# A product stage that centers and projects in one matmul per token on half of the array's rows

## The chip, the cores and the metric

The kernel runs on one core of one Trainium2 chip. The metric is the device time of one execution in microseconds (us); the lower the better. The times given are the median of several executions; the profile is of one execution, with its own time.

## The reference

The input `x` is 512 x 512 positions of 64 channels, in f32. Two layers are each added to their input.

Layer 0 first applies a group norm, then a triangle product over one axis of positions:

```python
xn = _ln(x, norm_w, norm_b)
left = xn @ left_w + left_b          # masked, times sigmoid(xn @ lgate_w + lgate_b)
right = xn @ right_w + right_b       # the same with its own weights
out = einsum('bkjd,bkid->bijd', left, right)
out = _ln(out, onorm_w, onorm_b)
out = out @ out_w + out_b
return out * sigmoid(xn @ ogate_w + ogate_b)
```

Layer 1 is a group norm, a two-dimensional Fourier transform cut to 12 x 12 modes, a complex matrix product over the channels for each mode, and the inverse transform.

The part that matters here is the line `out = _ln(out, onorm_w, onorm_b)` with the projection by `out_w` after it. For one token (one position with 64 channels), the layer norm subtracts the mean over its channels (centering), needs the sum of squares of the centered values, and divides by a root. Because the root is one number per token, the kernel projects the values first (with weights that have the centering folded in) and multiplies by the factor afterwards: `z = (token @ w_out) * rs + bias`, where `rs` is one over the root of the mean square of the centered token.

## The kernel before, in words

Rows whose mask is zero give nothing to the product, so the kernel compacts the rows with a mask to at most 256 (`compact`). Its stages follow one another:

- the masked rows are gathered, transposed for statistics and kept in SBUF (lines 640 to 690);
- they are normed and projected to left and right, 64 rows of the array at a time (L746), and written to DRAM;
- for each of the 64 channels, left and right are read back, transposed and multiplied (L835, L849); the product lies in the SBUF tile `places`, with 128 partitions for positions and, along the free axis, tokens of 64 channels;
- the stage with the change (lines 857 to 1141), described below;
- the layer 1 stage: modes, inverse transform and the sum, written to the output (lines 1143 to 1270).

The stage with the change works on groups of 64 tokens per partition, each group in 8 steps of 8 tokens per partition. `first` is 8: the first 8 groups (64 steps) hold the product and give `u`, the projected and normed product, which is written to DRAM (`u_d`). The 32 groups after them (256 steps) hold gathered tiles of `x`; they give the output gate, are multiplied by `u` or by the bias row, added to `x`, and stored. The names are: `transpose(s)` (L918) turns 8 tokens per partition with four transposes of 128 x 128 into the PSUM tile `t_ps`, and ScalarE copies it to the SBUF tile `xt_c` (L927; L929 for the later groups). In `xt_c` the array's rows 0 to 63 hold the channels of the even token of a pair and rows 64 to 127 those of the odd one. `times` (L931) multiplies such a tile, as the stationary operand, by a 128 x 128 matrix with two equal 64 x 64 blocks on the diagonal: four matmuls (L934). It is called twice per step: by `centered` (L937) with the matrix `center`, into `c_ps`, and by the loop (L1058) with `w_out`, into `w_ps`; the later groups use `center_x` and `gate_x`.

ScalarE squares `c_ps` (L944) into `sq_c`, of which there are two buffers of two steps each; VectorE sums the squares per token (L948), ScalarE takes the root once per group (`root`, L954), and VectorE the reciprocal (L1106). VectorE then multiplies `w_ps` by the factor into `z_t` (L1112) and, for two steps together, adds the bias, which is kept in PSUM (L1115); SyncE's queue stores `z_t` to `u_d` (L1118).

The order of the work is written out by hand in the loop at L1047: each engine takes its instructions in the order in which this loop issues them. A round `s` transposes step `s + 13` (`LEAD` is 13), projects step `s`, centers and squares step `s + 12`, sums the squares up to step `s + 11`, and scales step `s`. The loop begins at `s = -13`, so 13 rounds transpose and center before the first projection. The projection thus comes 12 rounds after the centering of the same tile, and for that time the tile waits in a ring of 15 buffers (L895). PSUM has eight banks: two for `t_ps`, two for `c_ps`, two for `w_ps`, one for sums and bias rows (`scratch`), one for the modes (`f_ps`).

```python
if s + LEAD < total_g:
    transpose(s + LEAD)
if 0 <= s < total_g:
    wps = times(ps_w, "w_ps", s, weights["out"] if k < first else gate_x)
if 0 <= s + LEAD - 1 < total_g:
    cps = centered(s + LEAD - 1)
...
if cps is not None:
    squared(s + LEAD - 1, cps)
```

Of the kernel before, what the change touches and what calls it, by code (L numbers as in the profile page):

```python
# [9 lines left out]
F32 = mybir.dt.float32  # L10
I32 = mybir.dt.int32
AF = mybir.ActivationFunctionType
ALU = mybir.AluOpType
AX = mybir.AxisListType
PSUM = bass.MemoryType.PSUM
DRAM = bass.MemoryType.DRAM

P = 128
N = 512
C = 64  # L20
# [26 lines left out]
def conv_preact_kernel(ctx: ExitStack, tc: tile.TileContext, t: dict):  # L47
    nc = tc.nc
    x, out = t["x"], t["out"]
# [12 lines left out]
    def load_const(name, shape):  # L62
        c = const.tile(shape, F32, name=name)
        nc.scalar.dma_start(c, t[name])
        return c

    ident = load_const("c_ident", [P, P])
    center = load_const("c_center", [P, P])
# [13 lines left out]
    with tc.tile_pool(name="ix", bufs=1) as xp, tc.tile_pool(  # L82
        name="ixp", bufs=1, space=PSUM
# [51 lines left out]
    weights, biases = {}, {}  # L135
# [476 lines left out]
    def compact(fc):  # L612
# [31 lines left out]
        with tc.tile_pool(name="xc", bufs=1) as cp:  # L644
            xc = cp.tile([P, K + 1, 2, C], F32, name="xc")
            with tc.tile_pool(name="f1", bufs=1) as sp, tc.tile_pool(name="f1x", bufs=2) as xp, tc.tile_pool(
                name="f1y", bufs=4
# [19 lines left out]
                for jc in range(NJ):  # L667
                    if jc % quarter == 0:
                        stats = sp.tile([P, 1, 16 * quarter, 6], F32, name="stats1c")
                    for r in range(4):  # L670
                        flat = xgs[jc][1][r].rearrange("p j c -> p (j c)")
                        for c in range(4):

                            ps = pt.tile([P, 4, P], F32, name="x_ps")
# [18 lines left out]
            with tc.tile_pool(name="fb", bufs=QB + 8) as gp, tc.tile_pool(name="fw", bufs=2) as wk, tc.tile_pool(  # L693
                name="fr", bufs=3
            ) as rp, tc.tile_pool(name="fg", bufs=1) as sp, tc.tile_pool(name="fo", bufs=2) as op, tc.tile_pool(
                name="fpt", bufs=2, space=PSUM
            ) as pt, tc.tile_pool(name="fpc", bufs=1, space=PSUM) as pc, tc.tile_pool(
                name="fpp", bufs=1, space=PSUM
# [13 lines left out]
                def centered(q):  # L712
                    cps = pc.tile([P, 8, C], F32, name="cc_ps")
                    for i in range(4):
                        nc.tensor.matmul(
                            cps[:, 2 * i : 2 * i + 2, :], gts[q][:, i * P : (i + 1) * P], center, start=True, stop=True
                        )
                    sq = wk.tile([P, 8, C], F32, name="sqc")
                    nc.scalar.activation(sq, cps, AF.Square)
                    k, n = divmod(q, QB)  # L720
                    if n == 0:
                        totals[k] = rp.tile([P, QB * 8], F32, name="total")
                    return sq, totals[k][:, 8 * n : 8 * n + 8]
# [26 lines left out]
                for q in range(-QB - 6, groups):  # L750
# [14 lines left out]
                    if live(QB + 5):  # L765
                        sq, total = centered(q + QB + 5)
# [22 lines left out]
        with tc.tile_pool(name="rb", bufs=2) as rp, tc.tile_pool(name="rbp", bufs=2, space=PSUM) as rps:  # L789
            for name in ("ogate", "out"):  # L790
                wide = rp.tile([P, P], F32, name="wide_" + name, tag="wide")
                nc.vector.tensor_copy(wide, biases[name].to_broadcast([P, P]))
                ps = rps.tile([P, C], F32, name="row_" + name, tag="row")
# [6 lines left out]
        center_x = fc.tile([P, P], F32, name="center_x")  # L800
        gate_x = fc.tile([P, P], F32, name="gate_x")
# [4 lines left out]
        with tc.tile_pool(name="tri", bufs=1) as trp:  # L806
# [17 lines left out]
            with tc.tile_pool(name="ti", bufs=4) as ip, tc.tile_pool(name="tt", bufs=3) as tp, tc.tile_pool(  # L824
                name="tpt", bufs=4, space=PSUM
            ) as ps_t, tc.tile_pool(name="tpo", bufs=3, space=PSUM) as ps_o:
                for c in range(C):
                    sides = []
                    for name, src in (("left", left_d), ("right", right_d)):
                        raw = ip.tile([P, 2, K], F32, name=name + "_raw")  # L830
# [15 lines left out]
                    ps = ps_o.tile([P, 2, K], F32, name="tri_c_ps")  # L846
# [10 lines left out]
            SIZE = 8  # L857
            LEAD = 13
            RING = 5
            first = K * 2 // 64  # L860

            units = [(jc, half) for jc in range(NJ) for half in ((1, 0) if jc < NJ - 1 else (0, 1))]
            total_g = (first + len(units)) * SIZE
            with tc.manual_schedule(), tc.tile_pool(name="late", bufs=1) as lp:
# [11 lines left out]
                def place(i):  # L876
                    return places[:, i * 64 * C : (i + 1) * 64 * C].rearrange("p (n c) -> p n c", c=C)
# [14 lines left out]

                    (nc.gpsimd if h == 3 else nc.sync).dma_start(modes_t, modes_d[h * P : (h + 1) * P])

                with tc.tile_pool(name="np_x", bufs=LEAD + 2) as tp, tc.tile_pool(name="np_q", bufs=2) as sqp, tc.tile_pool(  # L895
                    name="np_s", bufs=3
                ) as small, tc.tile_pool(name="oz", bufs=4) as zp, tc.tile_pool(
                    name="o1", bufs=1
                ) as s1, tc.tile_pool(name="np_t", bufs=2, space=PSUM) as ps_t, tc.tile_pool(
                    name="np_c", bufs=2, space=PSUM  # L900
                ) as ps_c, tc.tile_pool(name="np_w", bufs=2, space=PSUM) as ps_w, tc.tile_pool(
                    name="np_n", bufs=1, space=PSUM
                ) as ps_n, tc.tile_pool(name="opf", bufs=1, space=PSUM) as ps_f:
                    scratch = ps_n.tile([P, 4, P], F32, name="scratch")
                    sum_ps = [scratch[:, 3, i * G : (i + 1) * G] for i in range(2)]
                    bias_ps = {"out": scratch[:, 2, :C], "ogate": scratch[:, 2, C:]}
# [5 lines left out]
                    xts, rss, sqs, us, zs, fs, st = {}, {}, {}, {}, {}, {}, {}  # L912
                    last = len(units) - 1

                    def x_of(k):
                        return place(order[k % RING])

                    def transpose(s):  # L918
                        k, n = divmod(s, SIZE)
                        flat = (place(k) if k < first else x_of(k - first)).rearrange("p n c -> p (n c)")  # L920
                        tps = ps_t.tile([P, 4, P], F32, name="t_ps")
                        for i in range(4):
                            o = (8 * n + 2 * i) * C
                            nc.tensor.transpose(tps[:, i, :], flat[:, o : o + P], ident)  # L924
                        xts[s] = tp.tile([P, 4, P], F32, name="xt_c")
                        if k < first:
                            nc.scalar.copy(xts[s], tps)  # L927
                        else:
                            nc.scalar.activation(xts[s], tps, AF.Identity, bias=ab1[:, 2:3])  # L929

                    def times(pool, name, s, w):  # L931
                        ps = pool.tile([P, 8, C], F32, name=name)
                        for i in range(4):
                            nc.tensor.matmul(ps[:, 2 * i : 2 * i + 2, :], xts[s][:, i, :], w, start=True, stop=True)  # L934
                        return ps

                    def centered(s):  # L937
                        return times(ps_c, "c_ps", s, center if s < first * SIZE else center_x)

                    def squared(s, cps):  # L940
                        n = s % SIZE
                        if n % 2 == 0:
                            sqs[s // 2] = sqp.tile([P, 16, C], F32, name="sq_c")
                        nc.scalar.activation(sqs[s // 2][:, 8 * (n % 2) : 8 * (n % 2) + 8, :], cps, AF.Square)  # L944

                    def summed(s):
                        k, n = divmod(s, SIZE)
# [32 lines left out]
                    def finished():  # L980

                        z = zs.pop((last, 3))
                        made = [ps_c.tile([P, 8, C], F32, name="c_ps") for _ in range(2)]
                        for i, ps in enumerate(made):
                            u = bias_ps["out"].unsqueeze(1).to_broadcast([P, 8, C])
                            nc.vector.tensor_mul(ps, z[:, 8 * i : 8 * i + 8, :], u)
                        for i, ps in enumerate(made):
                            xr = x_of(last)[:, 48 + 8 * i : 56 + 8 * i, :]
                            nc.vector.tensor_add(xr, xr, ps)
# [57 lines left out]
                    for s in range(-LEAD, total_g + 2 * SIZE):  # L1047
                        k, n = divmod(s, SIZE)
# [5 lines left out]
                        if s + LEAD < total_g:  # L1054
                            transpose(s + LEAD)
                        wps = cps = None
                        if 0 <= s < total_g:
                            wps = times(ps_w, "w_ps", s, weights["out"] if k < first else gate_x)  # L1058
                            del xts[s]
                        if 0 <= s + LEAD - 1 < total_g:  # L1060
                            cps = centered(s + LEAD - 1)
# [3 lines left out]
                        if n % 2 == 0:  # L1065
                            i, c = (0, n // 2 - 1) if n >= 2 else (1, 3)
# [4 lines left out]
                        if cps is not None:  # L1071
                            squared(s + LEAD - 1, cps)
# [5 lines left out]
                        if n % 2 == 1:  # L1078
                            i, c = (0, (n - 3) // 2) if n >= 3 else (1, 3)
                            if held(i) and (v - i, c) != (last, 3):  # L1080
                                gated(v - i, c)
                            elif held(i):
                                finished()
                        else:
                            i, c = (0, (n - 4) // 2) if n >= 4 else (1, 2 + n // 2)
                            if held(i) and (v - i, c) != (last, 3):
                                added(v - i, c)
# [19 lines left out]
                        if wps is not None:  # L1107
                            c, odd = divmod(n, 2)
# [34 lines left out]
                with tc.tile_pool(name="lq", bufs=1) as qp, tc.tile_pool(name="lx", bufs=1) as xp:  # L1143
# [8 lines left out]
                    xts = {}  # L1152
# [18 lines left out]
                    with tc.tile_pool(name="sps", bufs=1, space=PSUM) as sps:  # L1171
# [8 lines left out]
                        for k in range(2):  # L1180
                            to = picks.rearrange("p m n k -> p m (n k)")[:, :, 12 * k : 12 * k + 33 * 11 + 1 : 33]
                            nc.vector.tensor_scalar(to, v[:, k], ab2[:, 0:1], None, ALU.mult)
                            h = slice(k * C, (k + 1) * C)
# [4 lines left out]
                        for m3 in range(3):  # L1188
                            for n in range(MODES):
                                for g in range(4):  # L1190
# [3 lines left out]
                                        start=(n == 0), stop=(n == MODES - 1), tile_position=(0, 32 * g),  # L1194
# [44 lines left out]
                    with tc.tile_pool(name="lpq0", bufs=2, space=PSUM) as pq, tc.tile_pool(  # L1239
                        name="lpt0", bufs=4, space=PSUM  # L1240
                    ) as pt:
                        back_columns(0, pq, pt, True)
                    with tc.tile_pool(name="lpq", bufs=1, space=PSUM) as pq, tc.tile_pool(
                        name="lpt", bufs=2, space=PSUM
                    ) as pt, tc.tile_pool(name="lps", bufs=4, space=PSUM) as pp:
                        for jc in range(NJ):
                            for b in range(4):
# [3 lines left out]
                                for g in range(4):  # L1251
                                    ps = pp.tile([P, JC, 16], F32, name="l_ps")
                                    h = slice(32 * g, 32 * g + M2)
                                    nc.tensor.matmul(  # L1254
                                        ps.rearrange("p j o -> p (j o)"), rinv[h, b, :], it[h],
                                        start=True, stop=True, tile_position=(32 * g, 0),
# [17 lines left out]
    with tc.If(rows_with_mask < K + 1) as few:  # L1274
        with tc.tile_pool(name="fconst", bufs=1) as fc:
            compact(fc)
# [65 lines left out]
```

## Time and profile before

| | us |
|---|---|
| median of 3 runs | 1890.53 |
| lowest and highest of them | 1883.09, 1893.93 |
| the profiled execution's own time | 1886.98 |
| its span, first to last instruction | 1885.2 |
| TensorE busy in it | 1683.2 (89%) |
| VectorE busy | 1458.5 (77%) |
| ScalarE busy | 922.0 (49%) |
| GpSimd busy | 873.0 (46%) |
| mean DMA rate | 248 GB/s |

PE is TensorE, PEld its weight loads, DVE VectorE, ACT ScalarE, POOL GpSimd and SP SyncE. A group of instructions is named by its line, engine, operation, and output and input tiles. The rounds that project the product run from about 685 to 827 us, those of the later groups from there to about 1541 us; the last stage, with the output, follows to the end. A matmul in f32 shows in the profile as two records, each with its own weight load; a transpose shows as one. The ends of matmul records are modelled, so starts tell more than durations.

### The profile page before, as it was taken

The page shows a single profiled execution, that of the slowest core. Times are in us where ns is not written, and L with a number is a line of the kernel's source. Part 1 is how long each engine was busy: PE and PEld are TensorE (multiplying, and loading weights), DVE is VectorE, ACT ScalarE, POOL GpSimd, SP SyncE. Part 2 cuts the span into 40 slices and gives each one's busy share as a digit, 9 for nine tenths or more (in the row PEclk, how much of TensorE's full clock was granted, in tenths as well). Part 3 has the DMA queues.
Part 4 walks back from the last instruction along what each step waited for, and adds up shares of the span by engine and source line. Part 5 has one row for each costly group of instructions (what it writes and reads, how often), then busy time and mean ns, then how long its engine had stood idle before and what let it go on. Part 6 is the DMA issues. An engine that isn't in the chain of part 4 may idle for free. (4 is left out here: it accounts for less than half of the span.)

```text
span 1885.2 us, 33737 instructions
## 1 busy us (share of the span) xinstructions
PE 1683.2 (89%) x11598; PEld 1350.9 (72%) x11598; DVE 1458.5 (77%) x2997; ACT 922.0 (49%) x1606; POOL 873.0 (46%) x678
## 2 busy tenths in 40 slices
PE   6779899998999999999999999999999956998873
PEld 5666666664788889998888888788888835664441
DVE  5989677777555568888999799979999994665552
ACT  3565555653222255567777677757767720111000
POOL 3655111111000000029999799979998982111110
PEclk9989899999999999999999899989999986555555
DMA  6999155556656534237777676767777589999999
GB/s 250 387 373 382 62 141 135 138 140 160 206 179 179 151 137 165 116 136 259 260 235 251 219 238 243 242 219 259 254 262 248 199 226 366 419 427 427 426 427 389
DMA packets 188868, 468.22 MB, mean 248 GB/s; under 512 B 35184, under 2 KB 134384, under 8 KB 147600
## 3 DMA queue, kind: packets, MB, share of 16 engines
q1 hardware_dynamic: 158192, 262.40, 41.4%
q0 software_dynamic: 27856, 202.19, 28.1%
q8 instruction: 94, 1.54, 0.3%
q10 hardware_dynamic: 2640, 1.38, 0.3%
q14 instruction: 86, 0.70, 0.1%
HBM read 278.13 MB, written 187.76 MB: 247 GB/s over the span
## 5 line engine op out<-in xcount | busy, mean ns | idle before, releaser
L934 PE MATMUL w_ps<-gate_x,xt_c 128*128 128x128 f32 x2048 | 281.9, 282 | 32.1 <-DVE z_t L1112 30.7
L978 POOL TENSOR_TENSOR places<-places,z_t 128x1024 f32<-128x1024 f32 x127 | 302.1, 2378 | 8.2
L934 PEld LDWEIGHTS w_ps<-gate_x,xt_c 128*128 128x128 f32 x2048 | 253.1, 195 | 49.1 <-DVE z_t L1112 48.6
L934 PE MATMUL c_ps<-center_x,xt_c 128*128 128x128 f32 x2048 | 276.3, 278 | 0.2
L934 PEld LDWEIGHTS c_ps<-center_x,xt_c 128*128 128x128 f32 x2048 | 252.5, 194 | 2.3 <-ACT xt_c L929 1.1
L944 ACT ACTIVATE sq_c<-c_ps 128x512 f32<-128x512 f32 x320 | 188.6, 590 | 104.3 <-PE c_ps L934 103.8
L1254 PE MATMUL l_ps<-places,rinv 24*128 24x512 f32 x512 | 209.7, 1128 | 31.7 <-DVE places L1261 25.7
L1112 DVE TENSOR_TENSOR z_t<-w_ps,rs_n 128x512 f32<-128x512 f32 x320 | 216.1, 675 | 23.0 <-PE w_ps L934 22.7
L1023 DVE BATCH_NORM_STATS2 stats2c<-places 128x6 f32<-128x128 f32 x1024 | 220.5, 279 | 8.1 <-POOL places L978 8.1
L948 DVE TENSOR_REDUCE scratch<-sq_c 128x16 f32<-128x1024 f32 x160 | 194.6, 1216 | 16.6 <-ACT sq_c L944 11.8
L1068 ACT ACTIVATE z_t<-z_t 128x1024 f32<-128x1024 f32 x128 | 135.5, 1058 | 142.0 <-DVE z_t L1115 117.7
L1115 DVE TENSOR_TENSOR z_t<-z_t,scratch 128x1024 f32<-128x1024 f32 x160 | 195.4, 1221 | 11.7 <-ACT rs_n L954 3.4
L1254 PEld LDWEIGHTS l_ps<-places,rinv 24*128 24x128 f32 x512 | 120.9, 304 | 115.4 <-DVE places L1261 73.1
L974 POOL TENSOR_TENSOR z_t<-z_t,bias_row_out 128x1024 f32<-128x1024 f32 x63 | 149.6, 2374 | 113.0 <-DMA places<-u_d 108.7
L924 PE MATMUL t_ps<-c_ident,places 128*128 128x128 f32 x1280 | 196.6, 277 | 1.3 <-DVE places L853 1.3
L1261 DVE TENSOR_TENSOR places<-places,l_ps 128x512 f32<-128x512 f32 x200 | 124.2, 683 | 86.5 <-DMA places<-x_h,dst_i 53.4
L929 ACT ACTIVATE xt_c<-t_ps,ab_xc 128x512 f32<-128x512 f32 x256 | 175.8, 687 | 23.8 <-PE t_ps L924 23.8
L924 PEld LDWEIGHTS t_ps<-c_ident,places 128*128 128x128 f32 x1280 | 148.9, 143 | 52.3 <-issue 52.3
L628 POOL DMA_INDIRECT places<-in_x,src_i x64 | 62.6, 978 | 261.9 <-PE c_ps L934 210.9
L974 POOL TENSOR_TENSOR z_t<-z_t,places 128x1024 f32<-128x1024 f32 x64 | 151.3, 2365 | 32.2 <-ACT z_t L1068 32.0
L678 DVE BATCH_NORM_STATS2 stats1c<-x_ps 128x6 f32<-128x512 f32 x256 | 156.0, 683 | 12.2 <-PE x_ps L677 11.3
L853 DVE SCALAR_TENSOR_TENSOR places<-tri_c_ps,slot_t,mask_s 128x256 f32<-128x256 f32 x128 | 73.1, 650 | 85.3 <-PE tri_c_ps L849 85.3
(203 smaller groups left out, 2641.9 us busy)
## 6 DMA issues: line engine op xcount, KB each, us to landing
x_h<-places SPq DMA_DIRECT2D x64, 1024.0 KB
out_x<-places SPq DMA_DIRECT2D x50, 1024.0 KB
places<-u_d SPq DMA_DIRECT2D x512, 64.0 KB
left_d<-o_c SPq DMA_DIRECT2D x64, 256.0 KB
right_d<-o_c SPq DMA_DIRECT2D x64, 256.0 KB
left_raw<-left_d SPq DMA_DIRECT2D x64, 256.0 KB
right_raw<-right_d SPq DMA_DIRECT2D x64, 256.0 KB
u_d<-z_t SPq DMA_DIRECT2D x32, 512.0 KB
```

Source lines behind the costliest of these rows:

```text
L678: nc.vector.bn_stats(stats[:, 0, 16 * (jc % quarter) + 4 * r + c, :], ps.rearrange("p i k -> p (i k)"))
L924: nc.tensor.transpose(tps[:, i, :], flat[:, o : o + P], ident)
L929: nc.scalar.activation(xts[s], tps, AF.Identity, bias=ab1[:, 2:3])
L934: nc.tensor.matmul(ps[:, 2 * i : 2 * i + 2, :], xts[s][:, i, :], w, start=True, stop=True)
L944: nc.scalar.activation(sqs[s // 2][:, 8 * (n % 2) : 8 * (n % 2) + 8, :], cps, AF.Square)
L948: nc.vector.tensor_reduce(totals[k % 2][:, 8 * (n - 1) : 8 * (n + 1)], sqs.pop(s // 2), AX.X, ALU.add)
L974: nc.gpsimd.tensor_mul(zs[k, c], zs[k, c], u)
L978: nc.gpsimd.tensor_add(xr, xr, zs.pop((k, c)))
L1023: nc.vector.bn_stats(st[k // 4][:, g, k % 4, :], x_of(k)[:, :, 2 * g : 2 * g + 2])
L1112: nc.vector.tensor_mul(z[:, 8 * odd : 8 * odd + 8, :], wps, rs)
L1115: nc.vector.tensor_add(z, z, bias.unsqueeze(1).to_broadcast([P, 16, C]))
L1254: nc.tensor.matmul(ps.rearrange("p j o -> p (j o)"), rinv[h, b, :], it[h], start=True, stop=True, tile_position=(32 * g, 0),)
```

## The change

For the 64 steps of the product, centering and projection of a token become one matmul. A matrix `both` of 128 x 128 is made once: in its rows 0 to 63, and again in its rows 64 to 127, it has the 64 x 64 centering block on the left and the 64 x 64 block of `w_out` on the right. `centered(s)` now takes each of the four pairs of tokens in `xt` and issues two matmuls for it, one with the array's rows 0 to 63 (the even token) and one with rows 64 to 127 (the odd token); each gives 128 columns, the token's centered channels beside its projected ones. The even tokens' results go to one PSUM bank, the odd ones' to another. The four banks that were `c_ps` and `w_ps` are one tile `banks`, of which two steps of the product use two banks each in turn; the later groups use them as before, two for centering and two for the gate.

ScalarE squares the left halves, as before, and then copies the right halves to SBUF, in token order. They lie in `ring`, 15 slots, which in the later groups holds the transposed tiles; the product's transposed tiles have two buffers of their own (`xt_y`), since they are done with after one round. In round `s` the product has no matmul of its own any more; VectorE multiplies slot `s % 15` of the ring by the factor. `finished` takes two of the banks for its tiles. The later groups compute as before.

```diff
-tp = pool "np_x", bufs=LEAD + 2;  ps_c = PSUM pool "np_c", bufs=2;  ps_w = PSUM pool "np_w", bufs=2
+tp = pool "np_x", bufs=1;  yp = pool "np_y", bufs=2;  ps_c = PSUM pool "np_c", bufs=1
+ring = tp.tile([P, LEAD + 2, N], F32, name="ring")
+banks = ps_c.tile([P, 4, N], F32, name="banks")
+both = lp.tile([P, P], F32, name="both")
+for h in range(2):
+    hs = slice(h * C, (h + 1) * C)
+    nc.vector.tensor_copy(both[hs, :C], center[hs, hs])
+    nc.vector.tensor_copy(both[hs, C:], weights["out"][hs, hs])
...
-xts[s] = tp.tile([P, 4, P], F32, name="xt_c")
+if k < first:
+    xts[s] = yp.tile([P, 4, P], F32, name="xt_y")
+else:
+    xts[s] = ring[:, s % (LEAD + 2)].rearrange("p (i k) -> p i k", i=4)
...
 def centered(s):
-    return times(ps_c, "c_ps", s, center if s < first * SIZE else center_x)
+    if s >= first * SIZE:
+        return times(s, s % 2, center_x)
+
+    ps = banks[:, 2 * (s % 2) : 2 * (s % 2) + 2].rearrange("p h (i c) -> p h i c", c=P)
+    for i in range(4):
+        for h in range(2):
+            hs = slice(h * C, (h + 1) * C)
+            nc.tensor.matmul(ps[:, h, i, :], xts[s][hs, i, :], both[hs], start=True, stop=True)
+    del xts[s]
+    return ps
...
-nc.scalar.activation(sqs[s // 2][:, 8 * (n % 2) : 8 * (n % 2) + 8, :], cps, AF.Square)
+sq = sqs[s // 2][:, 8 * (n % 2) : 8 * (n % 2) + 8, :]
+if s >= first * SIZE:
+    nc.scalar.activation(sq, cps, AF.Square)
+else:
+    by_half = lambda t: t.rearrange("p (i h) c -> p h i c", h=2)
+    nc.scalar.activation(by_half(sq), cps[:, :, :, :C], AF.Square)
+    nc.scalar.copy(by_half(raw(s)), cps[:, :, :, C:])
+
+def raw(s):
+    return ring[:, s % (LEAD + 2)].rearrange("p (n c) -> p n c", c=C)
...
-if 0 <= s < total_g:
-    wps = times(ps_w, "w_ps", s, weights["out"] if k < first else gate_x)
+if 0 <= s < first * SIZE:
+    wps = raw(s)
+elif 0 <= s < total_g:
+    wps = times(s, 2 + s % 2, gate_x)
     del xts[s]
```

The first three lines of the diff are shortened; the rest of the stage is unchanged.

More of the change, by code (lines that the diff above doesn't have):

```diff
@@ L893, in fetch @@
                     (nc.gpsimd if h == 3 else nc.sync).dma_start(modes_t, modes_d[h * P : (h + 1) * P])
-                with tc.tile_pool(name="np_x", bufs=LEAD + 2) as tp, tc.tile_pool(name="np_q", bufs=2) as sqp, tc.tile_pool(
+                with tc.tile_pool(name="np_x", bufs=1) as tp, tc.tile_pool(
+                    name="np_y", bufs=2
+                ) as yp, tc.tile_pool(name="np_q", bufs=2) as sqp, tc.tile_pool(
                     name="np_s", bufs=3
@@ L899, in compact @@
                 ) as s1, tc.tile_pool(name="np_t", bufs=2, space=PSUM) as ps_t, tc.tile_pool(
[L900 to L903, printed above, removed]
+                    name="np_c", bufs=1, space=PSUM
+                ) as ps_c, tc.tile_pool(name="np_n", bufs=1, space=PSUM) as ps_n, tc.tile_pool(name="opf", bufs=1, space=PSUM) as ps_f:
+                    ring = tp.tile([P, LEAD + 2, N], F32, name="ring")
[5 more added lines that the diff above has]
+                        nc.vector.tensor_copy(both[hs, C:], weights["out"][hs, hs])
                     scratch = ps_n.tile([P, 4, P], F32, name="scratch")
@@ L929, in transpose, with times @@
                             nc.scalar.activation(xts[s], tps, AF.Identity, bias=ab1[:, 2:3])
-                    def times(pool, name, s, w):
-                        ps = pool.tile([P, 8, C], F32, name=name)
+                    def times(s, bank, w):
+                        ps = banks[:, bank].rearrange("p (n c) -> p n c", c=C)
                         for i in range(4):
@@ L982, in finished @@
                         z = zs.pop((last, 3))
-                        made = [ps_c.tile([P, 8, C], F32, name="c_ps") for _ in range(2)]
+                        made = [banks[:, i].rearrange("p (n c) -> p n c", c=C) for i in range(2)]
                         for i, ps in enumerate(made):
```

## The prediction

> **What bounds the kernel now.** I read the table of stretches first, then the waits, then the order of time. The change lives in the product's groups, the 64 steps in which `w_ps` is made from `w_out`. Two rows of the stretches view bracket them: the lead-in of 13 steps (transposes and centering only), then the 64 steps. Columns after the stretch: its length; busy us and instructions (x) of PE, PEld, DVE, ACT, POOL; clock; DMA share; GB/s.
>
> ```profile
> 684.70:827.00 142.30, 142.30 (x1283) 142.30 (x1281) 122.00 (x136) 71.73 (x137) 2.81 (x3) 1.00 0.37 142
> 666.30:684.70 18.40, 17.32 (x152) 16.88 (x153) 7.05 (x9) 14.43 (x27) 2.92 (x3) 1.00 0.42 134
> ```
>
> TensorE never rests in the 64 steps: 1283 matmul records in 142.3 us are 0.111 us each, 20 per step (4 transposes; each f32 matmul shows as two records, so 8 for `w_ps` and 8 for `c_ps`), and 142.3/64 = **2.223 us a step**. VectorE has 20 us to spare. The waits view of this stretch says the same: both others wait for PE.
>
> ```profile
> ACT sq_c L944 <- PE c_ps L934: 70.8, 65, 1.2
> DVE z_t L1112 <- PE w_ps L934: 14.3, 24, 1.1
> ```
>
> In order of time (start, duration), one step of PE and of ScalarE:
>
> ```profile
> 746.59 0.60 PE L924 MATMUL t_ps<-c_ident,places 128*128 128x128 f32 x4
> 746.79 0.60 ACT L944 ACTIVATE sq_c<-c_ps 128x512 f32<-128x512 f32 x1 [1.15 <-PE c_ps L934]
> 747.02 1.06 PE L934 MATMUL w_ps<-w_out,xt_c 128*128 128x128 f32 x8
> 747.28 0.58 ACT L927 COPY xt_c<-t_ps 128x512 f32<-128x512 f32 x1
> 747.92 1.06 PE L934 MATMUL c_ps<-c_center,xt_c 128*128 128x128 f32 x8
> 748.81 0.60 PE L924 MATMUL t_ps<-c_ident,places 128*128 128x128 f32 x4
> ```
>
> Starts are 0.43, 0.90 and 0.89 apart: again 0.111 per record. ScalarE starts its second instruction 0.49 after its first. VectorE, by starts:
>
> ```profile
> 753.60 0.68 DVE L1112 TENSOR_TENSOR z_t<-w_ps,rs_n 128x512 f32<-128x512 f32 x1
> 754.20 0.54 DVE L1106 RECIPROCAL rs_n<-rs_n 128x64 f32<-128x64 f32 x1
> ...
> 757.97 0.68 DVE L1112 TENSOR_TENSOR z_t<-w_ps,rs_n 128x512 f32<-128x512 f32 x1
> 759.23 0.69 DVE L1112 TENSOR_TENSOR z_t<-w_ps,rs_n 128x512 f32<-128x512 f32 x1 [0.58 <-PE w_ps L934]
> ...
> 762.42 0.68 DVE L1112 TENSOR_TENSOR z_t<-w_ps,rs_n 128x512 f32<-128x512 f32 x1
> ```
>
> A pair of steps with the reciprocal takes 4.37 (753.60 to 757.97) and holds no wait. One without takes 4.45, but its second multiply starts 1.26 after the first where 0.60 is enough (753.60 to 754.20): 3.79 without the wait. Four pairs, one with a reciprocal: 3 x 3.79 + 4.37 = 15.74 per 8 steps, **1.967 us a step** is what VectorE needs. So only 0.256 us a step can be won before VectorE is the bound.
>
> **The trace has seen half rows.** An earlier stage projects 64 rows at a time into two banks (L746). Starts, then how many PE records (x) are live in short stretches:
>
> ```profile
> 241.21 1.06 PE L715 MATMUL cc_ps<-c_center,gc_t 128*128 128x128 f32 x8
> 242.20 1.13 PE L746 MATMUL sides_c<-xnc,w_sides 64*128 64x512 f32 x4
> 243.16 1.02 PE L746 MATMUL gates_c<-xnc,w_gates 64*128 64x512 f32 x4
> 244.12 0.66 PE L738 MATMUL rc_ps<-c_ident,rbc 128*128 128x128 f32 x4
> ```
> ```profile
> 242.65:242.70 0.05, 0.05 (x2) 0.00 (x0) 0.05 (x1) 0.05 (x1) 0.00 (x0) 1.00 0.83 164
> 242.70:242.75 0.05, 0.05 (x4) 0.02 (x2) 0.05 (x1) 0.05 (x1) 0.00 (x0) 1.00 0.00 0
> 243.10:243.15 0.05, 0.05 (x2) 0.00 (x0) 0.00 (x0) 0.05 (x1) 0.00 (x0) 1.00 0.58 82
> 243.15:243.20 0.05, 0.05 (x4) 0.04 (x2) 0.00 (x0) 0.05 (x1) 0.00 (x0) 1.00 2.85 492
> ```
>
> Two records start together, with two weight loads, every 0.45 us. A full-array record of the triangle (L849, 256 columns) takes 1.83/8 = 0.229 (groups start at 601.18, next work at 603.01), so 512 columns would be about 0.45 alone: the two halves run at once, and so do their weight loads. Entering half rows costs some 0.10 (242.20 - 241.21 = 0.99 against 0.89 for eight records), leaving them some 0.05 (rc_ps to its successor at 244.61 is 0.49 against 0.44).
>
> **What the Trainium skill says.** "TensorE: Matmul & The Clock Gate", Part 3, Packing small matmuls: matmuls in different row groups run concurrently. The rows above agree. "TensorEngine Tiling (Array Packing)", Key Properties and Gotcha 1: a change of tiling mode drains the array, and different row tiles must write different PSUM banks. The trace shows the first as those 0.10 and 0.05; the change obeys the second (`h` selects the bank), and L746 did too. "VectorE: DVE Perf Modes", the errata section: a f32 `tensor_tensor` from SBUF takes (N+151)/0.96 ns, 0.691 us at 512, though its table gives SBUF sources 62 cycles less than PSUM. The trace has 0.685 for this multiply with one PSUM source; it doesn't show it with two SBUF sources.
>
> **The change, part by part.** Two paces matter: p, that of the producers PE and ScalarE, and d, that of VectorE.
>
> *PE, p.* Removed: 16 full records a step. Added: 16 half-row records, in pairs, 8 slots. 4 x 0.111 + 8 x 0.111 + 0.15 for the two mode changes = 1.48. Unknown is the slot at 128 columns, where load and stream are equally long. Below 0.111 is excluded (the transposes, which load and stream the same 128 columns, don't go faster). Above, twice, 0.222, if the halves don't overlap. I take 0.111 to 0.12.
>
> *ScalarE.* Added: a second 128x512 eviction per step (raw projection, PSUM to the ring), like L927, 0.58 busy. It stands in ScalarE's queue ahead of the next transposed copy and the next square, for which PE and VectorE wait. Three starts 0.49 to 0.55 apart: about 1.5, plus a square root of 0.33 in 8 steps: 1.55. The square now reads two banks in strips of 64; same elements, taken at the same 0.60. So **p = 1.55**, hidden by VectorE in the steady steps, not in the lead-in.
>
> *VectorE, d.* The multiply reads the ring instead of PSUM. Bounds 0.62 (62 cycles less) to 0.75 (a blocked second read); I take 0.685, so **d = 1.967**. What it reads was written 12 steps before: no wait. The other new waits: ScalarE's write of raw step s+12 needs multiply s-3, and from step 51 the transposed copy of s+13 needs multiply s-2. Behind them queue squares and evictions, needed two steps later; the squares' two buffers already hold ScalarE to a lead of two steps, so I cost these at nothing; without that cover each would cost what VectorE lags, under a step.
>
> *Once.* Four 64-column copies for `both`, 0.23 each by L908, 0.92 us. They run from 666.2 while PE transposes and ScalarE copies; the first centering began at 667.79. Cost 0; at worst 0.9. No DMA is added; SP's stores of `u` and POOL's gathers stay in their order.
>
> *Sum.* The lead-in makes 12 centerings before step 0 at p instead of 1.33 (12 records). Steps 0 to 51 go at the slower of p and d. In steps 52 to 63 PE centers the next stage's groups (12 records, 1.33), so d holds. Change = 12(p - 1.33) + 52(max(p,d) - 2.223) + 12(d - 2.223) = 2.6 - 13.3 - 3.1 = -13.8. At step 64 the pace is PE's again (20 records); PE arrives there up to two steps ahead of VectorE: between 0 and -2, I take -0.5. **About -14 us.** VectorE's own order is late next. All later stages start that much sooner and keep their length: their work isn't changed, and the end (bound by DMA, share 1.0 from 1600 us on) depends on the stores that come before it. Against the profiled execution, 1886.98 (span 1885.2 and 1.8 around it): 1873. That run lies 3.5 below the median of 1890.53, so for the median: **1876.5**.
>
> Bounds of this case: multiply at 0.62 (-4), lead-in at 1.48 (-1), handover -1.5: -20. Multiply at 0.75 (+4), p = 1.7 (+2): -8.
>
> **Rivals.** (1) *PE or ScalarE still pace it*: slots of 0.18, or handovers among PE, ScalarE and two buffers that make p = 2.03: 12 x 0.70 - 52 x 0.19 - 3.1 = -4.6, so 1886. For it: three short stages in a ring with two buffers, and loads as long as streams. Against: in the lead-in PE kept 1.33 with two hops a step. (2) *The halves don't overlap*: slower. 16 x 0.111 + 0.44 + 0.15 = 2.37: 12 x 1.04 + 52 x 0.147 - 3.1 = +17, so 1907.5. It decides from p = 2.1, a slot of 0.19: the lead-in, paid in full, then eats the gain. Against: the pairs above. For: those had 512 columns to hide a load; here there are 128. (3) *The gain is taken back later*, 0, 1890: the next stage waits for something with its own time. Against: its loads of `u` follow this stage's last store, and its gathers are issued long before (from 670.99).
>
> **How the numbers follow.** Forecast 0.65, (1) 0.17, (2) 0.12, (3) 0.06. The forecast's own range is 1868 to 1883. The whole range goes to the upper cases, 1867 to 1890, leaving out (2) and little more. Half a per cent, 9.5 us, is about what a measurement here can tell from no change: that needs 1881. The forecast passes it nine times in ten, (1) seldom: faster 0.62, same 0.25, slower 0.13.
>
> **What would show it.** Right: 20 records a step with half of the matmuls starting in pairs; VectorE nearly without idle time between the first multiply and the next stage, 1.97 a step; ScalarE's wait for `c_ps` mostly gone; the lead-in some 2 to 4 us longer; the next stage's first `gate_x` matmul near 813 instead of 827. Wrong: records of `both` one after another at 0.111; VectorE waiting for squares; a multiply much off 0.68; or that first matmul early and the end not.

## The result, and the profile after

| | us |
|---|---|
| before, median of 4 runs | 1891.67 |
| after, median of 4 runs | 2179.41 (2177.66 to 2182.05) |
| ratio after to before | 1.1532, 95% interval 1.1493 to 1.1571 |
| the profiled execution after | 2182.05, span 2180.3 |

The change made the kernel 288 us slower; the forecast was 14 us faster. In the experiments below, the kernel before was timed again beside each group of runs, and its median is the second figure given. Ratios are of undisturbed runs: of the twelve runs of the last control, one took 6085 us and is left out of its ratio. The stretches view of the changed kernel, with the same columns as before, shows where: the lead-in, the product's rounds from their first multiply to the first gate matmul, and the later rounds.

```profile
662.90:693.70 30.80, 22.65 (x259) 18.10 (x260) 8.10 (x11) 21.31 (x40) 2.92 (x3) 1.00 0.30 103
693.70:837.20 143.50, 109.42 (x1179) 87.92 (x1175) 117.48 (x136) 96.81 (x188) 2.81 (x3) 1.00 0.34 136
837.20:1833.60 996.40, 739.45 (x5535) 618.58 (x5536) 686.30 (x1555) 513.41 (x737) 652.38 (x311) 0.95 0.52 172
```

The later rounds, in the kernel before:

```profile
827.00:1538.80 711.80, 668.83 (x5538) 590.04 (x5536) 667.32 (x1547) 501.05 (x737) 648.49 (x309) 0.98 0.71 238
```

The 256 later rounds, in which the same things are computed by the same instructions, take 996.4 us instead of 711.8: 3.89 a round instead of 2.78. That is +285. From the first centering matmul (667.8 before, 664.3 after) to the first gate matmul (827.0 and 837.2), the product's part takes 172.9 instead of 159.2: +14. The changed kernel reached its first centering 3.5 us sooner, so the two together, less these 3.5, are all of the 295.1 us between the two profiled spans. No engine is busy throughout the later rounds any more: TensorE is busy in 74% of them and VectorE in 69%, where both had 94% before. TensorE's granted clock in them, 0.95 against 0.98, differs far too little to explain that. The waits view of these rounds (who waited for whom, us in total, times, longest), after:

```profile
PEld banks L946 <- DVE z_t L1144: 316.5, 247, 3.3
...
DVE z_t L1144 <- ACT sq_c L967: 297.6, 159, 3.7
PE banks L946 <- DVE z_t L1144: 250.9, 196, 3.1
ACT sq_c L967 <- PE banks L946: 239.1, 101, 5.9
```

The second line is the strange one. VectorE's multiply (L1144) reads the gate's bank; ScalarE's square (L967) reads a centering bank. Neither makes anything for the other in that round, yet one waits for the other for 298 us. The same view of the kernel before has no such wait, and its gate matmuls wait for multiplies 30.7 us instead of 250.9:

```profile
PE w_ps L934 <- DVE z_t L1112: 30.7, 37, 2.0
```

In order of time, one later round after the change:

```profile
1103.57 1.16 PE L946 MATMUL banks<-gate_x,ring 128*128 128x128 f32 x8
...
1104.57 1.06 PE L946 MATMUL banks<-center_x,ring 128*128 128x128 f32 x8
...
1105.70 0.59 ACT L967 ACTIVATE sq_c<-banks 128x512 f32<-128x512 f32 x1
...
1106.32 0.69 DVE L1144 TENSOR_TENSOR z_t<-banks,rs_n 128x512 f32<-128x512 f32 x1 [2.03 <-ACT sq_c L967]
...
1107.07 0.60 PE L946 MATMUL banks<-gate_x,ring 128*128 128x128 f32 x3 [1.01 <-DVE z_t L1144]
```

Gate matmuls, centering matmuls, square, multiply, next gate matmuls: the square starts when the matmuls have ended, the multiply when the square has, the next gate matmuls when the multiply has, 3.50 us around in this round. Gate and centering lie in different banks of `banks`. The product's rounds show the same with two parties:

```profile
746.83 1.16 PE L957 MATMUL banks<-both,xt_y 64*128 64x128 f32 x16 [0.61 <-ACT ring L971]
...
748.04 0.60 ACT L970 ACTIVATE sq_c<-banks 128x512 f32<-128x512 f32 x1 [0.77 <-PE banks L957]
...
748.54 0.58 ACT L971 COPY ring<-banks 128x512 f32<-128x512 f32 x1
...
749.17 1.16 PE L957 MATMUL banks<-both,xt_y 64*128 64x128 f32 x16 [0.59 <-ACT ring L971]
```

The matmuls of a step wait for the eviction of the step before, although that reads the other two banks: 749.17 - 746.83 = 2.34 us a round, more than the 2.22 before.

### The profile page after: what moved, and what is told of

It is laid out like the page before. It is cut to its first block, busy times and chain, and to the rows that moved or that the text cites. A ratio compares the mean times of both kernels' runs of the same rounds, so it can differ in the third digit from the quotient of the medians.

```text
span 2180.3 us, 33824 instructions
## 1 busy us (share of the span) xinstructions
PE 1719.7 (79%) x11598; PEld 1326.5 (61%) x11598; DVE 1473.5 (68%) x3001; ACT 965.5 (44%) x1670; POOL 873.7 (40%) x678
## 5 line engine op out<-in xcount | busy, mean ns | idle before, releaser
L946 PE MATMUL banks<-gate_x,ring 128*128 128x128 f32 x2048 | 318.0, 302 | 257.2 <-DVE z_t L1144 250.9
L946 PEld LDWEIGHTS banks<-gate_x,ring 128*128 128x128 f32 x2048 | 267.1, 204 | 320.3 <-DVE z_t L1144 316.5
L1144 DVE TENSOR_TENSOR z_t<-banks,rs_n 128x512 f32<-128x512 f32 x256 | 176.2, 688 | 303.9 <-ACT sq_c L967 297.6
L946 PE MATMUL banks<-center_x,ring 128*128 128x128 f32 x2048 | 288.8, 287 | 3.7 <-ACT sq_c L967 3.1
L946 PEld LDWEIGHTS banks<-center_x,ring 128*128 128x128 f32 x2048 | 267.0, 204 | 6.5 <-ACT sq_c L967 5.7
L967 ACT ACTIVATE sq_c<-banks 128x512 f32<-128x512 f32 x256 | 150.6, 588 | 247.2 <-PE banks L946 247.1
L933 PE MATMUL t_ps<-c_ident,places 128*128 128x128 f32 x1280 | 201.5, 281 | 1.3 <-DVE places L853 1.3
L941 ACT ACTIVATE ring<-t_ps,ab_xc 128x512 f32<-128x512 f32 x256 | 175.6, 686 | 53.1 <-PE t_ps L933 53.0
L663 ACT COPY xc<-xg 128x128 f32 x352 | 105.0, 298 | 65.4 <-POOL xc L663 46.9
```

The costliest lines, as they stand in the source:

```text
L1144: nc.vector.tensor_mul(z[:, 8 * odd : 8 * odd + 8, :], wps, rs)
```

## The experiments

Two theories. **W**: the time went into waits that come from making four PSUM banks one tile; an engine's access waits for the access of another engine issued before it, whatever bank it is in. **H**: half-row matmuls, the second eviction or the ring are slow by themselves.

**Tiles of their own, all else kept.** The product's rounds get two tiles of two banks; when they are done, these are given back, and the later rounds get two one-bank tiles for centering and two for the gate, as in the kernel before.

```diff
-banks = ps_c.tile([P, 4, N], F32, name="banks")
+pools = {"pair": <PSUM pool, bufs=2>}        # at step 64: <close it>, pools "c" and "w", bufs=2 each
-ps = banks[:, 2 * (s % 2) : 2 * (s % 2) + 2].rearrange("p h (i c) -> p h i c", c=P)
+ps = pools["pair"].tile([P, 2, 4, P], F32, name="pair")
-ps = banks[:, bank].rearrange("p (n c) -> p n c", c=C)
+ps = pools[pool].tile([P, 8, C], F32, name=name)
```

> The changed kernel with its matmuls, ring and copies, but the PSUM banks in tiles of their own: two tiles of two banks for the product's rounds, and, once these are given back, two one-bank tiles for centering and two for the gate, as in the kernel before. Theory W (the time went into waits that come from putting four banks into one tile: each engine's access waits for the one issued before it, whatever bank it is in): the 256 later rounds fall back from 3.89 to 2.79 us, the product's rounds from 2.33 to 1.97, and the whole is near the forecast, 1876 us, 10 to 20 below the kernel before. Theory H (half-row matmuls, the second eviction or the ring are slow by themselves): the product's rounds stay near 2.33 us, and the whole stays above 1890; if the ring or bank traffic also slows the later rounds, above 2100.

Measured: 1879.63 against 1893.73, ratio 0.9933 (0.9913 to 0.9953), **14.1 us faster than before**. The stretches are the lead-in to the first multiply, the product's rounds by VectorE's multiplies, and the later rounds from their first gate matmul (TensorE is ahead of VectorE there, so the last two overlap):

```profile
667.00:689.43 22.43, 21.61 (x259) 17.95 (x260) 7.73 (x8) 20.71 (x40) 2.92 (x3) 1.00 0.42 142
689.43:814.51 125.08, 111.57 (x1208) 93.94 (x1205) 119.76 (x137) 98.06 (x192) 2.81 (x3) 0.97 0.40 158
809.40:1524.50 715.10, 669.23 (x5538) 590.40 (x5536) 670.29 (x1552) 501.51 (x738) 648.71 (x309) 0.98 0.71 237
```

125.08/64 = 1.954 us a round in the product, 2.79 in the later rounds. The half rows, the eviction and the ring are all still there. H falls. In the waits view of the later rounds the multiply's wait for the square is gone, and gate matmuls wait for multiplies about as long as in the kernel before:

```profile
PE w_ps L947 <- DVE z_t L1149: 32.0, 35, 2.4
```

**The kernel before, with its four banks made one tile.**

```diff
-ps = pool.tile([P, 8, C], F32, name=name)
+ps = banks[:, bank].rearrange("p (n c) -> p n c", c=C)     # c: bank s % 2, w: bank 2 + s % 2
```

> The kernel before with one edit: the two tiles of c_ps and the two of w_ps become one tile of four banks, each step using the same bank as it would have. No half rows, no second eviction, no ring. Theory W: the later rounds go from 2.79 to about 3.9 us (+284), the product's rounds from 2.22 to about 3.6, as projection, centering, square and multiply follow one another (+90): 2250 to 2280 us. Theory H: no change, 1890.

Measured, one run: 2257.56, 364 us above the kernel before. No part of the change is in it but the tile. The order of time has the same ring of four, now in the product's rounds too:

```profile
800.74 1.16 PE L935 MATMUL banks<-w_out,xt_c 128*128 128x128 f32 x8 [0.97 <-DVE z_t L1113]
801.74 1.06 PE L935 MATMUL banks<-c_center,xt_c 128*128 128x128 f32 x8
...
802.83 0.60 ACT L945 ACTIVATE sq_c<-banks 128x512 f32<-128x512 f32 x1 [2.39 <-PE banks L935]
...
803.46 0.69 DVE L1113 TENSOR_TENSOR z_t<-banks,rs_n 128x512 f32<-128x512 f32 x1 [0.26 <-ACT sq_c L945]
804.20 1.16 PE L935 MATMUL banks<-w_out,xt_c 128*128 128x128 f32 x8 [0.97 <-DVE z_t L1113]
```

3.46 us a round instead of 2.22. In its later rounds, 998.7 us long, multiplies wait for squares 300.7 us in all, 159 times: nearly the 297.6 us and 159 times of the changed kernel. The merged tile alone is enough for the loss.

**The kernel before, with its 15 SBUF tiles made one ring.**

```diff
-xts[s] = tp.tile([P, 4, P], F32, name="xt_c")
+xts[s] = ring[:, s % (LEAD + 2)].rearrange("p (i k) -> p i k", i=4)
```

> The kernel before with one edit: the 15 tiles in which transposed values wait become 15 slots of one SBUF tile. Theory W for PSUM alone: no change, 1890 within 5 us. Theory R (one tile in SBUF is also taken as one thing by the waits): each transposed copy waits for the projection issued before it, and slower by tens of us at least, above 1930.

Measured: 1893.92 against 1893.73, ratio 0.9999 (0.9984 to 1.0014). One SBUF tile with slots costs nothing here, and its gate matmuls wait for multiplies 28.1 us, no longer than before. So the trouble is with the PSUM tile.

**The changed kernel with two tiles of two banks.**

```diff
-banks = ps_c.tile([P, 4, N], F32, name="banks")
+pairs = [ps_c.tile([P, 2, N], F32, name=f"pair{i}") for i in range(2)]   # later rounds: c in one, w in the other
```

> The changed kernel with its four banks as two tiles of two banks: in the later rounds centering uses one of them and the gate the other; in the product's rounds each step has one. If the waits are by tile: the later rounds no longer chain centering to the gate, but the gate's matmuls of a step wait for VectorE's multiply of the step before, and centering for the square of the step before: 2.9 to 3.3 us a round, 1910 to 2020 in all. If the waits are by bank inside a tile of two, and only the four-bank tile is treated as one: near 1876.

Measured: 1939.33 against 1893.73, ratio 1.0243 (1.0217 to 1.0269). The stretches view has the later rounds at 778.9/256 = 3.04 us, and the waits view of them has one chain gone and one left:

```profile
812.70:1591.60 778.90, 673.68 (x5537) 590.45 (x5536) 683.71 (x1558) 520.08 (x738) 652.67 (x311) 0.98 0.66 220
```
```profile
PEld pair L946 <- DVE z_t L1144: 122.2, 77, 3.1
PE pair L946 <- DVE z_t L1144: 103.5, 73, 2.9
```

The multiply no longer waits for the square, which is in the other tile. But gate matmuls wait 103.5 us in all for multiplies, against 32.0 where each bank is a tile. In order of time:

```profile
1001.56 0.68 DVE L1144 TENSOR_TENSOR z_t<-pair,rs_n 128x512 f32<-128x512 f32 x1
1002.30 1.16 PE L946 MATMUL pair<-gate_x,ring 128*128 128x128 f32 x8 [1.60 <-DVE z_t L1144]
1003.49 0.69 DVE L1144 TENSOR_TENSOR z_t<-pair,rs_n 128x512 f32<-128x512 f32 x1
```

What the gate matmuls at 1002.30 write, the multiply at 1003.49 reads; they waited for the multiply at 1001.56, of the step before, which reads the other bank of the same tile. So the unit of these waits is the tile, with two banks as with four. The other wait that was expected, of centering for the square of the step before, hardly shows (under 0.5 us in all).

**One part at a time.** The kernel of the first experiment with only the product's rounds in one tile of four banks, then with only the later rounds in one:

```diff
 # product's rounds only                                   # later rounds only
-ps = pools["pair"].tile([P, 2, 4, P], ...)               -ps = pools[pool].tile([P, 8, C], ...)
+ps = banks[:, 2 * (s % 2) : 2 * (s % 2) + 2]...          +ps = pools["all"][:, bank]...
```

> The kernel of e1 with only the product's rounds in one tile of four banks, as the change has them; the later rounds keep tiles of their own. Theory W (one tile's accesses wait for each other): the product's half-row matmuls wait for the eviction of the step before, 2.33 us a round; between the first centering and the first gate matmul 173 us instead of 142, the later rounds 2.79 as before: 1910 us. Rival (the tile of four banks only hurts where two engines read it, so not here): as e1, 1880.

> The kernel of e1 with only the later rounds in one tile of four banks; the product's rounds keep their two tiles of two. Theory W: 3.89 us a later round, 256 x (3.89 - 2.79) = 281 above e1, 2150 to 2165 us; with e5 it adds up to what the change cost. Rival (the two parts are coupled, one of them being slow only behind the other): below 2100.

Measured: the first 1904.80 against 1890.91, ratio 1.0070 (1.0048 to 1.0093), that is +13.9; the second, one run, 2152.04, that is +261. Against the -14.1 with tiles apart, the product's tile costs 28 and the later rounds' tile 275. -14 + 28 + 275 = 289; the change cost 288. The account closes, so the two parts are not coupled; and the product's part costs its 28 though only ScalarE reads the tile there, so two reading engines aren't needed for it.

**Whole rows in place of half rows.** As the first experiment, but the product's rounds project and center with full-array matmuls, in the same round as the half rows did.

```diff
-for i in range(4):
-    for h in range(2):
-        nc.tensor.matmul(ps[:, h, i, :], xts[s][hs, i, :], both[hs], ...)
+for h, w in enumerate((weights["out"], center)):
+    for i in range(4):
+        nc.tensor.matmul(ps[:, h, i, :], xts[s][:, i, :], w, ...)
```

> The kernel of e1 with the half-row matmuls replaced by full-array ones in the same round: four by w_out into one bank of the pair, four by center into the other; square and eviction each read one bank. Theory F (the gain of e1 comes from the two halves running at once): 20 records of 0.111 us, 2.22 a round for TensorE also in the lead-in; against e1 12 x (2.22 - 1.68) + 52 x (2.22 - 1.95) = +20 us, 1900. Rival (the gain comes from the ring, that is from VectorE no longer waiting for TensorE within a round): near e1, 1880 to 1885.

Measured: 1897.75 against 1890.91, ratio 1.0039 (1.0023 to 1.0055), 6.8 slower than before. Half rows against whole rows are thus worth 14.1 + 6.8 = 21 us, as expected. The gain comes from the halves running at once. The rest of the change alone loses, since it puts the projection into the lead-in: that takes 28.5 us (665.3 to 693.8) instead of 18.5, and the product's rounds win back only 3.0 (139.8 from the first multiply to the first gate multiply, instead of 142.8).

**What bounds the repaired kernel: the bias on GpSimd.** As the first experiment, but GpSimd adds the product's bias, from SBUF.

```diff
-nc.vector.tensor_add(z, z, bias_ps["out"]...)
+nc.gpsimd.tensor_add(z, z, rows_of["out"].unsqueeze(1).to_broadcast([P, 16, C]))
```

> The kernel of e1 with the bias of the product's rounds added by GpSimd, from the bias row in SBUF, instead of by VectorE from PSUM. Theory D (VectorE's own order sets the product's rounds of e1 at 1.95 us): VectorE needs about 1.3 us without the addition, and TensorE's 1.68 us a round sets the pace: 64 x (1.95 - 1.68) = 17 us below e1, 1862. Rival (GpSimd's addition of 2.4 us per two rounds holds up VectorE's multiply, which now has both inputs in SBUF): 1.85 a round or more, 1874 or above. Rival (something else sets the pace of e1): no change, 1880.

Measured: 1872.37 against 1890.91, ratio 0.9893 (0.9866 to 0.9919): 18.5 faster than before, 4 more than the first experiment's 14.1 and not the 17 more that I had expected. The rival with GpSimd was right in its cause and its pace, 1.86 us a round (686.9 to 805.8 for 64), and just missed its total of 1874 or above. In order of time, a GpSimd addition and two multiplies of VectorE (on one line):

```profile
744.43 2.37 POOL L1152 TENSOR_TENSOR z_t<-z_t,bias_row_out 128x1024 f32<-128x1024 f32 x1 [1.69 <-DVE z_t L1149]
...
745.35 2.60 DVE L1149 TENSOR_TENSOR z_t<-ring,rs_n 128x512 f32<-128x512 f32 x2
```

Two multiplies take 2.60 us where they took 1.28. The first of them alone takes 2.00, to 747.35, and so ends 0.55 after GpSimd's addition, which ends at 746.80.

**The factor in PSUM.** With the reciprocal written to a free part of the PSUM tile `scratch`, the multiply has only one input in SBUF. It was run with the bias on GpSimd, and as a control with the bias on VectorE.

```diff
-nc.vector.reciprocal(rss[k + 1], rss[k + 1])
+inv = scratch[:, (k + 1) % 2, C : 2 * C] if k + 1 < first else rss[k + 1]
+nc.vector.reciprocal(inv, rss[k + 1]);  rss[k + 1] = inv
```

> The kernel of e8 with the reciprocal of the product's groups written to PSUM, so that VectorE's multiply has one input in SBUF and one in PSUM. Theory P (in e8 the multiply waits for GpSimd's addition because both need the second way into SBUF): the multiply is back at 0.68 us while GpSimd adds, the product's rounds take TensorE's 1.68 us, 9 to 12 us below e8, 1860 to 1863. Rival (two engines reading SBUF at once disturb each other whatever the operands): the multiply stays near 2 us in every second round, and the whole at 1872.

> The kernel of e1 with the reciprocal of the product's groups written to PSUM, and the bias still added by VectorE: the control to e9. Theory P: GpSimd is nearly idle in these rounds, so nothing changes, 1879 within 4 us. Rival (a PSUM operand makes the multiply itself faster or slower, or its tile brings new waits): a change of more than 4 us.

Measured with GpSimd: **1862.17 against 1888.43, ratio 0.9862 (0.9836 to 0.9889)**, the fastest version here, 26 us below the kernel before. Its multiplies take 0.69 us beside GpSimd's additions; these two, 1.28 together, run while an addition does (753.26 to 755.62):

```profile
754.55 1.28 DVE L1151 TENSOR_TENSOR z_t<-ring,scratch 128x512 f32<-128x512 f32 x2
```

Eight rounds (reciprocal to reciprocal, 751.84 to 765.27) take 13.43, 1.68 each, TensorE's pace.

The control missed: 1886.83 against 1888.43, ratio 0.9994 (0.9977 to 1.0011), some 12 us worse than the first experiment. The timeline of VectorE in the control says why:

```profile
746.96 0.69 DVE L1151 TENSOR_TENSOR z_t<-ring,scratch 128x512 f32<-128x512 f32 x1
748.03 0.69 DVE L1151 TENSOR_TENSOR z_t<-ring,scratch 128x512 f32<-128x512 f32 x1 [0.38 <-ACT rs_n L989]
```

The multiply now reads `scratch`, and so waits for ScalarE's root, which reads another group's sums in the same tile. That wait is 0.38 us in eight rounds. Eight rounds take 16.82 us (752.05 to 768.87, by reciprocals) where the first experiment needs 15.59 (748.56 to 764.15), which makes 10 us in 64 rounds, so most of it lies elsewhere: in VectorE's own order. The multiply starts 1.26 us after the start of the sum that writes `scratch`, where it was 1.14, and the reciprocal 0.72 after the multiply, where it was 0.60: each now starts only after the one before it has ended. These are again waits inside one PSUM tile, but the tile is one bank, so this run can't tell tile from bank. The fast version has them too (0.85 us for the root at 749.01); there VectorE has time to spare.

## Why the prediction was wrong

What failed is one step, that the later stages keep their length, and under it a term put at nothing without a reason: the four banks made one tile, which cost 275 us there and 28 in the product's rounds. The parts in turn:

- **TensorE bounds the product's rounds, VectorE is next at 1.967 us.** Right: 1.954 with tiles apart, and with VectorE relieved, TensorE's own pace appears.
- **The halves run at once at 128 columns.** Right: 21 us between whole and half rows. The pace was mis-sized: I took 1.48 for TensorE. With tiles apart it is 1.68: the four transposes take 0.59 until the first half-row matmul (747.14 to 747.73, 0.15 more than the 0.44 before) and the 16 half-row records 1.09 until the next transpose, where I had 0.89 and 0.05. VectorE hides this but for the lead-in.
- **The multiply at 0.685 from SBUF, the eviction at 0.58, the square unchanged.** Right: 0.682, 0.579 and 0.597 in the medians of the changed kernel.
- **The lead-in, +2.6.** From the first centering to the first multiply 22.4 instead of 18.5 (667.79 to 686.30): +3.9, from the pace above. The first gate multiply came at 814.51 instead of 829.12. From the first multiply to that one, 125.1 instead of 142.8: -17.7, where the forecast had -16.9. The forecast of -14 for the change is met at -14.1 once its tiles are apart, in part by luck, as these two misses pull opposite ways.
- **"All later stages start that much sooner and keep their length: their work isn't changed."** This step failed, and with it the sum. Their work is not changed; their tiles are. The later rounds lost 275 us, as the run with only their banks in one tile shows, to waits that I didn't list.
- **"The other new waits."** I listed two waits, on slots of the ring, by what reads and writes the same data, and costed them at nothing. In the first experiment ScalarE does wait for multiplies before it fills a slot, 7.0 us in all, five times, but the product's rounds still take what VectorE needs. I didn't list the waits among the four banks: the diff's line `banks = ps_c.tile([P, 4, N])` stands in my description of the change, and got no cost. In the product's rounds these waits made the producers' pace 2.34, from a chain of matmuls, square and eviction.
- **The rivals.** None was this one. Rival (1) came nearest in form ("a ring with two buffers"), but it left the later rounds alone. Rival (2), the slower one, was ruled out by the run with whole rows. Rival (3) had the place, the next stage, but another cause, and no more than the gain to lose.

The Trainium skill, "PSUM — Partial Sum Buffer", section "PSUM bank collisions raise a hardware error", says that two engines must not be in one bank and quadrant at once, reads included, while different banks may be used side by side. The trace of the kernel before agrees with the second: here a multiply reads a `w_ps` bank until 686.98 while a square has read a `c_ps` bank since 686.76.

```profile
686.30 0.68 DVE L1112 TENSOR_TENSOR z_t<-w_ps,rs_n 128x512 f32<-128x512 f32 x1
686.76 0.60 ACT L944 ACTIVATE sq_c<-c_ps 128x512 f32<-128x512 f32 x1 [1.15 <-PE c_ps L934]
```

What the runs add is that, in these programs, the order was kept between engines on a PSUM tile of several banks as a whole, so that banks that could be used side by side weren't when they shared a tile. Two experiments show it by their waits (one tile in the kernel before, two tiles of two banks); the factor in PSUM lies within one bank and can't. The banks themselves don't need these waits: with tiles apart, the same work runs without them. What puts them into the program is not shown, and whether every layout of a tile would be treated so was not tried.

## What to carry to other kernels

Where a diff merges PSUM tiles, cost the merge by itself: write down, in the order of the loop, every engine that touches the tile in a round, and add their times as one chain; if it is longer than the round, expect it as the new pace. Give banks that different steps or readers use at the same time tiles of their own; two banks that one step fills and one engine reads, as in the first experiment, can share one. And a stage that a diff "leaves as before" keeps its time only if its buffers are left too.

## What the runs showed of the hardware that I had not expected

GpSimd's addition holds up a VectorE multiply with both inputs in SBUF: with the bias on GpSimd, a multiply that meets an addition takes 2.0 us instead of 0.68, and 0.69 again with one input in PSUM. The Trainium skill, "SBUF — State Buffer", section "SBUF: two separate sides", says that such an operation shares a pair of ports with GpSimd, which one holds for a whole instruction; both runs agree. I had named a "blocked second read" in the bound of the multiply, and put it at 0.75 us; where GpSimd works, it is nearly three times that.

Half-row matmuls of 128 columns cost more than their slots: 16 records, 8 pairs, take 1.09 us until the next transpose, 0.136 a pair with the change of mode in it, against 0.111 for a full-array record.
